# Layer 3's queries and keys: from one level of Strassen's method on two samples to two levels on four

## The chip, the cores and the metric

One core of a Trainium2 chip runs the whole kernel. Time is the device time of that core in microseconds (us). A profiled execution gives the trace behind every view; three plain executions give the times. TensorE is called PE in the views (PEld are its weight loads), VectorE DVE, ScalarE ACT, GpSimd POOL and the queue that issues the DMAs SP.

## The reference, cut to what matters

128 samples, each with x of 128 nodes by 512 features and an adjacency matrix of 128 by 128, pass four layers; each ends in `x = layernorm(x + layer(x, adj))`. All is fp32.

- Layer 0 mixes neighbours through a transition matrix in two steps, with three weight matrices.
- Layer 1 is a hypergraph convolution through 1024 hidden features.
- Layer 2 builds attention weights from one score per node, then multiplies by W.
- Layer 3, the one that is edited, is masked attention with 8 heads of 64:

```
q, k, v = x@Wq.T + bq, x@Wk.T + bk, x@Wv.T + bv      # per sample, 128 x 512 each
scores  = (q @ k.T) * 64**-0.5 * (adj + adj)         # per head, 128 x 128
ctx     = softmax(scores) @ v
x       = layernorm(x + ctx@Wo.T + bo)
```

## The kernel before, in words

The kernel works on pairs of samples (U = 2, 64 pairs). Three stages follow each other: `layer0` (four samples at a time), `layer1` and `layer23` (a pair at a time). A stage is a generator: each `yield` in it ends a step. `layer` (L1233) runs the steps of pair k with `plan.key = start + k + w`, w from the lists `WHEN0`, `WHEN1`, `WHEN2` (L35 to L38), so one unit of the key is one pair and several pairs are under way at once.

Nothing is issued while the steps run. `Plan.add` (L181) records each operation with its engine, an estimated duration and what it depends on. `Plan.order` (L227) then places all operations: PE takes the ready operation with the lowest key, the other engines the one that is due first (`deadlines`, L342). It also gives each tile its place: `slots` (L398) says how many places of a kind there are, and `later` which places are made out of others once those are done for good. `emit` writes the instructions out in that order, so all of them carry one line, L364. Each engine executes its list strictly in that order.

The kinds of tiles: "bank" is one of eight PSUM banks (two of them called t0 and t1), "four" holds 2 x 512 numbers per partition, "sq" 2 x 130, "row" 512, "col" 12, "out" layer 0's results. `first` is one large SBUF tensor that holds layer 0's weights and later w2 and the weights of q and k ("w28") and W ("w14").

`strassen` (L538) multiplies a 2 x 2 arrangement of blocks by another with 7 products in place of 8 (Winograd's form). `operands` (L523) makes four sums of the left blocks on POOL, `combine` (L469) the sums of the weights once. Three banks are used: al gathers four of the products one after the other, be two, ga one, and after each product an eviction adds the bank to a result in SBUF (`take`). With `flip` the weights stand still in PE and the left block moves, so that the result comes out transposed.

In `layer23`, a pair goes through these steps: x2 and adj are loaded; layer 2's weights F are made and go through DRAM to be transposed; GT = x2.T F; the product with W and the layer norm give x3, which stays in SBUF in the tile of x2 and also goes through DRAM, to come back as xT; POOL makes the sums for q, k and v, and adds the bias bo to x3; q and k come out of one `strassen` with `nk = 2, nh = 512, flip=True`: 7 products, each of 512 columns in 8 matmuls of 128 x 128 x 128; v, scores, softmax, ctx and the product with Wo follow, whose evictions start from x3.

`layer0` already multiplies four samples by two levels of the method: 49 products of 386 columns. Its sums of left blocks and its seven inner `strassen` calls are written out in that function.

Of the kernel before, what the change touches and what calls it, by code (L numbers as in the profile page):

```python
# [17 lines left out]
P = 128  # L18
D = 512
# [9 lines left out]
SQS = 13  # L29
COLS = 48  # L30
ROWS = 8
# [6 lines left out]
WHEN2 = (-2.4, -2.0, -1.45, -1.15, -.7, 0, .35, .7, 1.35, 1.7)  # L38
LAG1, LAG2 = 1, -.5
RAMP = 0, 0, .2, 6  # L40
# [19 lines left out]
SPARE, AHEAD = 3, 6  # L60
SIZE = {"four": U * D, "sq": U * (P + 2), "bank": D, "col": 12, "row": D, "w28": 7168, "w14": 3584,
        "w7": 7 * QW, "out": U * 4 * QW, "t0": D, "t1": D}
# [99 lines left out]
class Plan:  # L162
# [64 lines left out]
    def order(self, urgent=None):  # L227
# [40 lines left out]
        def look(e):  # L268
# [3 lines left out]
            for k, t in ready[e].items():  # L272
# [7 lines left out]
                for kind, tiles in new.items():  # L280
                    s, m = slots[kind], len(tiles)
                    spare = 0
                    if not all(tile in line[kind][-m:] for tile in tiles):
                        spare = SPARE if all(tile in line[kind][-m - AHEAD:] for tile in tiles) else math.inf
                    if len(s) < m + (min(spare, 3) if kind == "bank" else spare):
                        break
                    t = max(t, sorted(s)[m - 1][0])
                else:
                    can.append((rank[k], t, k))
                    if t < soonest:  # L290
                        soonest = t
# [81 lines left out]
def kernel(  # L373
# [16 lines left out]
    first = const.tile([P, 7 * SIZE["w7"]], FP, name="first")  # L390
    outs = [const.tile([P, SIZE["out"]], FP, name=f"out{k}") for k in range(OUTS)]
    places = {"w7": [first[:, k * SIZE["w7"]:(k + 1) * SIZE["w7"]] for k in range(7)], "out": outs}
    at = 3 * SIZE["w7"], 7 * SIZE["w7"] - SIZE["w14"]
    places["w28"] = [first[:, k:k + SIZE["w28"]] for k in (0, at[0])]
    places["w14"] = [first[:, at[1]:]]
    later = {("w28", 0): [("w7", k) for k in range(3)], ("w28", 1): [("w7", k) for k in range(3, 6)],
             ("w14", 0): [("w7", k) for k in range(5, 7)]}
    slots = {"w7": 7, "out": OUTS, "w28": 0, "w14": 0, "sq": SQS, "col": COLS, "row": ROWS, "bank": 6, "t0": 1, "t1": 1,  # L398
             "four": BUFS}
# [6 lines left out]
    for k, t in enumerate(outs):  # L406
        for c in range(SIZE["out"] // SIZE["four"]):
            later["four", len(places["four"])] = [("out", k)]
            places["four"].append(t[:, c * SIZE["four"]:(c + 1) * SIZE["four"]])
# [55 lines left out]
    def seven(nk, nh):  # L465

        return tile_of("w28" if nk * nh == 1024 else "w14", 7, nk, nh)
# [8 lines left out]
    def load_blocks(W, left, right, by_blocks=False, dma=sp.dma_start):  # L476


        for half, at in ((left, B11), (right, B12)):
            to = W[:, at:at + 2].rearrange("p g c f -> p (g c) f")  # L480
            if by_blocks:
                with plan.together():
                    for k in range(4):
                        dma(to[k * Q:(k + 1) * Q], half.rearrange("(k c a) f -> k a c f", k=4, a=Q)[k],
                            run=half.shape[1], parts=Q)
            else:
                dma(to, half.rearrange("(c p) f -> p c f", p=P))
        combine(W)

    def load_T(W, srcs, nk, nh, with_stage=None, by_blocks=False, scale=1.0):  # L490

        n = 0
        for src in srcs:
            for o in range(src.shape[0] // P):
# [11 lines left out]
                for g in range(src.shape[1] // D):  # L506
# [5 lines left out]
                    for c0 in range(0, C, nk):  # L512
# [4 lines left out]
                        ac.mul(W[:, blk, k0:k0 + m, at:at + P], pt[:, c0:c0 + m],  # L517
                               scale if src is srcs[0] else 1.0)
                n += P
                yield  # L520
        combine(W)
# [173 lines left out]

    def spread_pair(srcs):
# [34 lines left out]
    def prepare0():  # L731
# [56 lines left out]
        flat = [w.rearrange("p j o f -> p (j o f)") for w in W]  # L788
        for to, a, b in ((T1, B12, B11), (T2, B22, T1), (T3, T2, B11), (N4, B21, T2)):
            (po if to in (T3, N4) else ve).tensor_tensor(flat[to], flat[a], flat[b], OP.subtract)  # L790
# [23 lines left out]
    def layer0(i0):  # L814
# [10 lines left out]

        base = plan.key

        def sums(to, L):

            S1, S2, S3, S4 = (to[:, k] for k in range(4))  # L830
            po.tensor_tensor(S1, L[:, :, 1, 0], L[:, :, 1, 1], OP.add)
            po.tensor_tensor(S3, L[:, :, 0, 0], L[:, :, 1, 0], OP.subtract)
            po.tensor_tensor(S2, S1, L[:, :, 0, 0], OP.subtract)
            po.tensor_tensor(S4, L[:, :, 0, 1], S2, OP.subtract)

        halves_of = [t.rearrange("p u (j c) n -> p j u c n", j=2) for t in xT]
        (A11, A12), (A21, A22) = [[t[:, j] for j in range(2)] for t in halves_of]
        lefts = []

        def give(L, n):  # L840
            to = tile_of("four", 4, n, P)
            sums(to, L)
            lefts.extend((L[:, j], to[:, :, j]) for j in range(n))

        give(halves_of[0], 2)
        two = [tile_of("four", 2, U, 2, P) for _ in range(2)]
        (S2, S1), (S4, S3) = [[t[:, j] for j in range(2)] for t in two]
        po.tensor_tensor(S1, A21, A22, OP.add)
        po.tensor_tensor(S2, S1, A11, OP.subtract)
        plan.key = base + .5  # L850
        give(two[0], 2)
        plan.key = base + 1
        po.tensor_tensor(S4, A12, S2, OP.subtract)
        po.tensor_tensor(S3, A11, A21, OP.subtract)
        give(two[1], 2)
        plan.key = base + 1.5
        give(halves_of[1][:, 1:], 1)
# [5 lines left out]
        def quarters(r, half):  # L863

            return [R[r][:, b, 2 * half + n] for b in range(U) for n in range(2)]

        def fresh(d, bs):

            def put(d, b):
                def run(p):  # L870
                    ac.copy(d[:, P:], p[:, P:])
                    add(d[:, :P], p[:, :P], b, OP.add)
                return run
            d11, d12, d21, d22 = d
            return {"p1": put(d11, bs[:, 0]), "c11": lambda p: add(d11, p, d11, OP.add),
                    "v": put(d12, bs[:, 1]), "c12": lambda p: add(d12, p, d12, OP.add),
                    "p5": put(d22, bs[:, 1]), "c22": lambda p: add(d22, p, d22, OP.add),
                    "c21": put(d21, bs[:, 0])}

        C11, C12, X, Y = quarters(0, 0), quarters(0, 1), quarters(1, 0), quarters(1, 1)  # L880
        sides = [[R[r][:, b, 2 * h:2 * h + 2] for b in range(U)] for r, h in ((0, 1), (1, 0), (1, 1))]
        for k, (j, take) in enumerate((
                (B11, fresh(X, bias[:, 0])), (B21, biased_take(C11, X)), (T2, biased_take(X, X)),
                (T1, fresh(Y, bias[:, 1])), (B22, biased_take(C12, C12)), (T3, biased_take(X, X)),
                (N4, biased_take(X, X)))):
            plan.key = base + .28 * k
            L, S = lefts[k]
            strassen((L[:, 0, :1], L[:, 0, 1:], L[:, 1, 1:], [S[:, i:i + 1] for i in range(4)]), WT["0"][j], 1, QW,
                     take)
            if j in (T1, T3):  # L890
                for b in range(U):
                    po.tensor_tensor(sides[j == T3 and 2][b], sides[1][b], sides[2][b], OP.add)
# [41 lines left out]
    b1_b = [row() for _ in range(2)]  # L934
    b2h = row()
    bw2 = row()
# [25 lines left out]
    def layer1(i0):  # L962
# [23 lines left out]
        K = sq(M)  # L986
# [76 lines left out]
    def prepare2():  # L1063
# [15 lines left out]
        ve.tensor_copy(bkT, pt[:, C:2 * C])  # L1079
        yield  # L1080
        WT["w"] = seven(2, h)
        load_blocks(WT["w"], w[:, :h], w[:, h:])
        yield
        WT["qk"] = seven(2, D)
        yield from load_T(WT["qk"], [wq, wk], 2, D, None, True, 0.25)
# [17 lines left out]
    def layer23(i0):  # L1103
        x2 = load_rows(x2d[i0 // U])
        A = load_adj(i0)
        yield
        s2 = col(U)
        for b in range(U):
            dot(s2[:, b:b + 1], x2[:, b], wa_b)
        deg = col(U)  # L1110
        ve.tensor_reduce(deg, A, AX.X, OP.add)
        pt = spread_pair([s2[:, b:b + 1].to_broadcast([P, P]) for b in range(U)])
        F = sq()
        for b in range(U):
            ac.activation(F[:, b], pt[:, b * P:(b + 1) * P], AF.Tanh, bias=s2[:, b:b + 1])
        ac.activation(F, F, AF.Prelu, alpha=0.1)
        ac.activation(F, F, AF.Exp, scale=8.0)
        r = col(U)
        for b in range(U):
            ve.scalar_tensor_tensor(F[:, b], F[:, b], 1.0, A[:, b], op0=OP.mult, op1=OP.mult,  # L1120
                                           accum_out=r[:, b:b + 1])
        ve.reciprocal(r, r)
        for b in range(U):
            po.tensor_scalar(F[:, b], F[:, b], r[:, b:b + 1], deg[:, b:b + 1], op0=OP.mult, op1=OP.mult)
# [163 lines left out]
```

## Time and profile before

| what | value |
|---|---|
| median of 3 runs | 5561.65 us (5557.36 to 5562.09) |
| the profiled execution's own time | 5560.11 us |
| its span | 5558.2 us |
| PE busy | 5489.4 us, 28697 records |
| DVE, ACT, POOL busy | 3872.5, 2121.4, 3370.9 us |
| DMA | 650.24 MB, mean 117 GB/s |
| layers 2 and 3 | first store of the output at 3266 us, last at 5554 us |

The span is from the first instruction to the last in the profiled execution. A busy share is an average over three stages with different loads, so the shares are to be read stage by stage. Matmul ends are modelled, and an fp32 matmul leaves two records for itself and two for its weight loads. Idle time of an engine other than PE costs nothing unless PE waits for it.

### The profile page before, as it was taken

What the parts mean: (1) busy time and instruction counts of PE and PEld (TensorE: products, weight loads), DVE (VectorE), ACT (ScalarE), POOL (GpSimd) and SP (SyncE); (2) the same over time, 40 slices, a digit from 0 to 9 for tenths busy, and PEclk for the clock granted to TensorE, in tenths of its full rate; (3) what the DMA queues carried; (4) which work ended last, traced back from release to release, by engine and by line L of the source; (5) the groups of instructions that cost most, each with busy time, mean ns of one, the idle gap of its engine ahead of it and who ended that gap; (6) DMA issues with size and microseconds to landing.
All of it is one profiled execution on the core that took longest, in us unless ns stands there. A gap on an engine that the chain in (4) does not pass through costs nothing.

```text
span 5558.2 us, 87851 instructions
## 1 busy us (share of the span) xinstructions
PE 5489.4 (99%) x28697; PEld 4082.3 (73%) x28697; DVE 3872.5 (70%) x8130; ACT 2121.4 (38%) x5327; POOL 3370.9 (61%) x5080
## 2 busy tenths in 40 slices
PE   8999999999999999999999999999999999999999
PEld 4555555555666666666666798999999999999998
DVE  6888888878666666666665666767677777776766
ACT  2333333334333333333333333433333333333433
POOL 6767777766666666666666545555555555555554
PEclk9999999999999999999999999999999999999999
DMA  3333333334444443344444434434443344334442
GB/s 89 105 93 103 96 97 103 99 105 138 137 132 115 119 115 115 110 116 119 119 119 119 131 108 130 132 113 122 133 131 115 121 133 133 116 120 131 131 127 91
DMA packets 717680, 650.24 MB, mean 117 GB/s; under 512 B 259739, under 2 KB 571043, under 8 KB 717222
## 3 DMA queue, kind: packets, MB, share of 16 engines
q1 hardware_dynamic: 715718, 641.99, 39.0%
q8 instruction: 229, 3.75, 0.3%
q10 hardware_dynamic: 1504, 2.62, 0.2%
q14 instruction: 229, 1.88, 0.1%
HBM read 360.20 MB, written 284.16 MB: 116 GB/s over the span
## 4 chain that ended last, share of the span: by engine, by line
PE 85%; DMA 4%; DVE 4%; POOL 2%; issue 1%; SPq 1%; ACT 1%; DVEq 0%; ACTq 0%; POOLq 0%
PE bank L364 66%; PE t L364 19%; DVE out L364 2%; SPq L364 1%; DMA four<-x 1%; POOL four L364 1%; DMA four<-h 1%; DMA out<-h 1%; DVE col L364 1%; DVE four L364 1%; POOL out L364 1%; POOL col L364 1%; ACT out L364 1%; DVE sq L364 0%; DMA four<-in_x_dram 0%
## 5 line engine op out<-in xcount | busy, mean ns | idle before, releaser
L364 PE MATMUL bank<-first,four 128*128 128x386 f32 (+1 forms) x5372 | 1614.5, 447 | 21.7 <-DVE first L364 5.1
L364 PEld LDWEIGHTS bank<-first,four 128*128 128x128 f32 x5372 | 993.3, 190 | 583.3 <-DVE out L364 120.3
L364 DVE TENSOR_TENSOR out<-bank,out 128x386 f32<-128x386 f32 (+2 forms) x1785 | 913.6, 531 | 491.1 <-PE bank L364 423.5
L364 PE MATMUL bank<-four,four 128*64 128x128 f32 (+3 forms) x2508 | 598.1, 399 | 0.0
L364 POOL TENSOR_TENSOR four<-four 128x256 f32<-128x256 f32 (+2 forms) x502 | 360.4, 732 | 287.1 <-ACT four L364 187.0
L364 ACT COPY four<-bank 128x256 f32<-128x256 f32 (+1 forms) x494 | 233.3, 474 | 779.3 <-PE bank L364 775.8
L364 POOL TENSOR_TENSOR out<-out 128x772 f32<-128x772 f32 (+2 forms) x212 | 330.3, 1564 | 255.4 <-DVE out L364 214.7
L364 PEld LDWEIGHTS bank<-four,four 128*128 128x128 f32 (+2 forms) x2508 | 338.5, 172 | 188.2 <-issue 155.0
L364 DVE TENSOR_TENSOR four<-bank,four 128x256 f32<-128x256 f32 (+1 forms) x509 | 221.0, 437 | 346.0 <-PE bank L364 339.4
L364 POOL TENSOR_TENSOR four<-four,four 128x256 f32<-128x256 f32 (+2 forms) x566 | 447.1, 792 | 10.7
L364 POOL TENSOR_TENSOR out<-out,row 128x512 f32<-128x512 f32 x208 | 264.9, 1277 | 275.7 <-PE bank L364 116.0
L364 PE MATMUL bank<-four,first 128*128 128x128 f32 x3536 | 422.3, 275 | 0.7 <-DVE four L364 0.7
L364 PEld LDWEIGHTS bank<-four,first 128*128 128x128 f32 x3536 | 414.4, 192 | 7.1 <-DVE four L364 1.1
L364 ACT ACTIVATE out<-out,col,col 128x512 f32<-128x512 f32 (+1 forms) x290 | 280.1, 985 | 341.7 <-POOL col L364 331.4
L364 ACT COPY out<-bank 128x258 f32<-128x258 f32 (+2 forms) x484 | 194.4, 404 | 566.0 <-PE bank L364 451.2
L364 PE MATMUL bank<-first,out 128*128 128x256 f32 (+1 forms) x1748 | 407.5, 380 | 0.5 <-DVE out L364 0.3
L364 PE MATMUL bank<-four,out 128*128 128x512 f32 (+3 forms) x1500 | 402.8, 416 | 2.6 <-DVE four L364 2.6
L364 POOL TENSOR_SCALAR col<-col 128x1 f32<-128x1 f32 (+1 forms) x704 | 189.4, 273 | 351.9 <-DVE col L364 315.6
L364 ACT ACTIVATE four<-four,col,col 128x512 f32<-128x512 f32 (+1 forms) x350 | 285.4, 820 | 302.4 <-POOL col L364 267.1
L364 POOL TENSOR_TENSOR col<-col,neghalf 128x1 f32<-128x1 f32 x640 | 387.4, 609 | 17.0
L364 PE MATMUL bank<-out,four 128*128 128x256 f32 (+3 forms) x1768 | 363.0, 363 | 8.2 <-DVE out L364 6.2
L364 PEld LDWEIGHTS bank<-first,out 128*128 128x128 f32 x1748 | 330.5, 190 | 51.5 <-DVE out L364 2.9
(213 smaller groups left out, 10368.3 us busy)
## 6 DMA issues: line engine op xcount, KB each, us to landing
h<-out SPq DMA_DIRECT2D x472, 128.0 KB, 2.5
four<-S SPq DMA_DIRECT2D x76, 512.0 KB, 4.4
S<-four SPq DMA_DIRECT2D x75, 512.0 KB, 2.9
out<-h SPq DMA_DIRECT2D x69, 512.0 KB, 4.6
four<-in_x_dram SPq DMA_DIRECT2D x512, 64.0 KB, 2.1
four<-in_x_dram SPq DMA_DIRECT2D x62, 512.0 KB, 3.8
x1d<-four SPq DMA_DIRECT2D x62, 512.0 KB, 2.8
out<-x1d SPq DMA_DIRECT2D x59, 512.0 KB, 6.1
```

The costliest lines, as they stand in the source:

```text
L364: call(*map(real, args), **{n: real(a) for n, a in kw.items()})
```

## The change

The queries and keys of layer 3 are made for four samples (two pairs) at a time by two levels of the method: an outer level over the pair index and the two halves of q and k, an inner level in each of its seven products. That is 49 products with one contraction block of 128 and 256 columns, where two pairs had 14 products with two blocks and 512 columns.

- `lefts` and `twice` are layer 0's code, moved out into functions that layer 0 and `layer23` call. `lefts` makes the sums of both levels on POOL. `twice` runs the seven inner `strassen` calls; two POOL additions form the shared part of the results after the products T1 and T3.
- The weights of q and k lie in seven tiles "q7". `load_T(twice=True)` combines them at the inner level, `combine_once_more` at the outer.
- Evictions that carry a bias are two ACTIVATEs of 128 columns with the bias as a column, on ScalarE; the other 41 of 49 add the bank to the result on VectorE. The bias bk is stored as bk - bq.
- x3 is stored to DRAM (`x3d`) after layer 2 and reloaded for the product with Wo; bo is added after the reload. The results of that product are written over x3.
- `layer23` runs on two pairs, with a key per pair inside a step (`each`), and the attention is a function of its own, with times from `WHENV`, `WHENS`, `WHENP` and `WHENO`.
- Places: 8 in place of 13 sq, 32 of 48 col, 4 of 8 row and one "row1" for layer 1's rows; layer 1's K has a kind of its own with 4 places. After layer 1 the places of w2, row1 and K become fours. W is loaded into fours by `prepare_w`; Wv's and Wo's load (`prepare3`) has a later key.

```diff
-SQS = 13
-COLS = 48
-ROWS = 8
+SQS = 8
+COLS = 32
+ROWS = 4
+KS = 4
...
-WHEN2 = (-2.4, -2.0, -1.45, -1.15, -.7, 0, .35, .7, 1.35, 1.7)
-LAG1, LAG2 = 1, -.5
-RAMP = 0, 0, .2, 6
+WHEN2 = (-2.4, -2.0, -1.45, -1.15, -.7, .3, .5, 2)
+WHENV, WHENS, WHENP, WHENO = (.9, 1.9), (2.2, 3.2), (3, 4), (3.5, 4.5)
+LAG1, LAG2 = 1, -.25
+SOFT = .2
+RAMP = 0, 0, .05, 4
...
+    def lefts(xT, step=.5):
+        base = plan.key
+        def sums(to, L):
+            S1, S2, S3, S4 = (to[:, k] for k in range(4))
+            po.tensor_tensor(S1, L[:, :, 1, 0], L[:, :, 1, 1], OP.add)
+            po.tensor_tensor(S3, L[:, :, 0, 0], L[:, :, 1, 0], OP.subtract)
+            po.tensor_tensor(S2, S1, L[:, :, 0, 0], OP.subtract)
+            po.tensor_tensor(S4, L[:, :, 0, 1], S2, OP.subtract)
...
+        give(halves_of[0], 2)
+        two = [tile_of("four", 2, U, 2, P) for _ in range(2)]
+        (S2, S1), (S4, S3) = [[t[:, j] for j in range(2)] for t in two]
+        po.tensor_tensor(S1, A21, A22, OP.add)
+        po.tensor_tensor(S2, S1, A11, OP.subtract)
+        plan.key = base + step
+        give(two[0], 2)
+        plan.key = base + 2 * step
+        po.tensor_tensor(S4, A12, S2, OP.subtract)
+        po.tensor_tensor(S3, A11, A21, OP.subtract)
+        give(two[1], 2)
+        plan.key = base + 3 * step
+        give(halves_of[1][:, 1:], 1)
+        return found
+
+    def twice(left, W, width, quarters, sides, fresh, step, flip=False):
+        base = plan.key
+        C11, C12, X, Y = (quarters(r, half) for r in range(2) for half in range(2))
+        for k, (j, take) in enumerate((
+                (B11, fresh[0](X)), (B21, biased_take(C11, X)), (T2, biased_take(X, X)), (T1, fresh[1](Y)),
+                (B22, biased_take(C12, C12)), (T3, biased_take(X, X)), (N4, biased_take(X, X)))):
+            plan.key = base + step * k
+            L, S = left[k]
+            strassen((L[:, 0, :1], L[:, 0, 1:], L[:, 1, 1:], [S[:, i:i + 1] for i in range(4)]), W[j], 1, width,
+                     take, flip=flip)
+            if j in (T1, T3):
+                for d, v, y in zip(sides(*((0, 1), (1, 1))[j == T3]), sides(1, 0), sides(1, 1)):
+                    po.tensor_tensor(d, v, y, OP.add)
...
     def layer23(i0):
...
+            strassen(ops, WT["w"], 2, D // 2, normed(biased_take(halves(x2), halves(x2)), x2))
+
+            loads.append(through_dram(x2.rearrange("p b (k w) -> p b k w", k=4), f"x3{i}"))
+            x3ds.append(held(f"x3d{i}"))
+            sp.dma_start(x3ds[-1], x2)
...
-        strassen(ops, WT["qk"], 2, D, {
-            "p1": op(qT[:, 0], bqb), "c11": op(qT[:, 0], qT[:, 0]), "v": op(kT[:, 0], bkb),
-            "c12": op(kT[:, 0], kT[:, 0]), "p5": op(kT[:, 1], bkb), "c22": op(kT[:, 1], kT[:, 1]),
-            "c21": op(qT[:, 1], bqb)}, flip=True)
+        left = lefts(xT)
+        yield
+        qk = [[four().rearrange("p u (f n) -> p u f n", n=P) for _ in range(2)] for _ in range(2)]
...
+                    def run(p):
+                        for f in range(2):
+                            ac.activation(d[:, f * P:(f + 1) * P], p[:, f * P:(f + 1) * P], AF.Identity,
+                                          bias=bias[:, 2 * q + f:2 * q + f + 1])
...
+        twice(left, WT["qk"], 2 * P,
+              lambda r, half: [qk[r][half][:, b, 2 * m:2 * m + 2].rearrange("p f n -> p (f n)")
+                               for b in range(U) for m in range(2)],
+              lambda r, half: [qk[r][half][:, b].rearrange("p f n -> p (f n)") for b in range(U)],
+              [fresh(bqT), fresh(bkT)], .25, True)
+        for r in range(2):
+            plan.key = base + WHENV[r]
+            strassen(operands(*blocks(xT[r])), WT["v"], 2, D // 2, plain_take(*halves(vs[r])))
+        yield
+        for r, i in enumerate(both):
+            attention(i, As[r], *qk[r], vs[r], x3ds[r], base, r)
...
-        t = four()
-        yield
-        strassen(ops, WT["o"], 2, D // 2, normed(biased_take(halves(t), halves(x3)), t))
-        sp.dma_start(out[i0:i0 + U].rearrange("b p f -> p b f"), t)
+        plan.key = base + WHENO[r]
+        x3 = load_rows(x3d)
+        for b in range(U):
+            po.tensor_tensor(x3[:, b], x3[:, b], bo_b, OP.add)
+        strassen(ops, WT["o"], 2, D // 2, normed(biased_take(halves(x3), halves(x3)), x3))
+        sp.dma_start(out[i0:i0 + U].rearrange("b p f -> p b f"), x3)
```

## Prediction, before the result was known

> **What bounds the kernel now.** I read four views in this order: the page, the busy times of two stretches, the order of time inside one pair, and the groups by form. First the page (busy time, share of the span, instructions) and the chain that ended last:
>
> ```profile
> PE 5489.4 (99%) x28697; PEld 4082.3 (73%) x28697; DVE 3872.5 (70%) x8130; ACT 2121.4 (38%) x5327; POOL 3370.9 (61%) x5080
> PEclk9999999999999999999999999999999999999999
> PE 85%; DMA 4%; DVE 4%; POOL 2%; issue 1%; SPq 1%; ACT 1%; DVEq 0%; ACTq 0%; POOLq 0%
> ```
>
> TensorE is busy 99% of the span at full clock, and it is 85% of the chain. The average hides three stages, so next come the windows: one inside layer 0, which already uses 49 products per four samples, and one inside the stage that the change edits (layers 2 and 3, from about 3200 us to the end).
>
> ```profile
> core 0: us, PE busy (x) PEld busy (x) DVE busy (x) ACT busy (x) POOL busy (x), PEclk, DMA share, GB/s
> 500.00:1000.00 500.00, 497.20 (x1478) 267.15 (x1477) 399.30 (x936) 191.50 (x423) 358.22 (x499) 1.00 0.34 99
> 3300.00:5300.00 2000.00, 1990.30 (x15016) 1818.31 (x15015) 1422.42 (x2929) 777.90 (x2594) 1107.59 (x1623) 1.00 0.41 126
> ```
>
> In the edited stage TensorE idles 9.7 us of 2000 (0.49%), with DVE at 71% and POOL at 55%. Layer 0 idles 2.8 of 500 (0.56%) with DVE at 80% and POOL at 72%. So in both places matmul time is wall time. The stores of the output leave 36.77 us apart (mean over 48 pairs), 73.54 us per four samples. The timeline gives the price of one matmul:
>
> ```profile
> 4214.67 1.03 PE L364 MATMUL bank<-four,out 128*128 128x256 f32 x4
> 4215.54 1.03 PE L364 MATMUL t<-out,out 128*128 128x256 f32 x4
> 4226.90 1.95 PE L364 MATMUL bank<-out,first 128*128 128x128 f32 x16
> 4228.69 3.74 PE L364 MATMUL bank<-four,first 128*128 128x128 f32 x32
> 4232.26 1.95 PE L364 MATMUL bank<-out,first 128*128 128x128 f32 x16
> ```
>
> Each fp32 matmul leaves two records. From start to start, 16 records of 128 columns take 1.79 us (4226.90 to 4228.69) and 32 take 3.57, so one 128-column matmul costs 0.223 us. A 256-column one costs 0.87/2 = 0.433 us.
>
> **The change part by part.**
>
> *TensorE.* Before, a pair of samples has 7 products, each of 4 (f) x 2 (c) = 8 matmuls of 128 columns: 56, or 112 per four samples. After, four samples have 49 products of 2 matmuls of 128 columns: 98. The kind is the same (a 128x128 weight load, 128 moving columns). So 14 x 32 groups = 448 matmuls go (the two programs hold 14565 and 14117): 448 x 0.2234 = 100.1 us, on the path. No other matmul is added or removed.
>
> *VectorE and ScalarE.* Rows for the evictions and sums (mean ns is the figure behind the busy time):
>
> ```profile
> L364 DVE TENSOR_TENSOR four<-bank,four 128x256 f32<-128x256 f32 x475 | 197.6, 419 | 320.8 <-PE bank L364 314.2 <-POOL sq L364 2.0 <-POOL out L364 0.8
> L364 DVE TENSOR_TENSOR out<-bank,bqT 128x512 f32<-128x512 f32 x64 | 44.2, 690 | 69.7 <-PE bank L364 69.6
> L364 ACT ACTIVATE sq<-bank,col 128x128 f32<-128x128 f32 x210 | 66.2, 363 | 115.8 <-PE bank L364 114.0 <-ACT four L364 1.7
> L364 POOL TENSOR_TENSOR four<-four,four x566: 452/730/1287, 15.1 to 5532.5; 128x256 f32<-128x256 f32 x136, 128x512 f32<-128x512 f32 x31, 128x128 f32<-128x128 f32 x22
> L364 POOL TENSOR_TENSOR out<-out 128x512 f32<-128x512 f32 x60 | 76.4, 1275 | 26.0 <-DVE out L364 18.2 <-DMA out<-x1d 6.4 <-DMA sq<-in_adj_dram 0.8
> ```
>
> Removed per four samples: 14 evictions of 512 (0.690). Added: 41 of 256 on DVE (0.419) and, for the eight evictions that carry a bias, 16 ACTIVATEs of 128 (0.363). DVE: 17.2 - 9.7 = +7.5 us. It has 52.3 now (1422.4/2000 x 73.54), so it comes to 59.8 of a period of 73.54 - 3.13 = 70.4 us, 85%. ACT: 28.6 + 5.8 = 34.4 us, 49%.
>
> *POOL.* Added per four samples: 12 sums of 256 (0.73), 4 of 128 (0.459, mean of that shape in the trace), 4 of 512 (1.275) for the left operands, and 4 of 512 for the shared halves of q and k: 8.8 + 1.8 + 5.1 + 5.1 = +20.8 us. POOL has 40.7 now, so it comes to 61.5 of 70.4 us, 87%. No stage of the trace runs POOL or DVE this full; layer 0 is nearest. These loads are shadowed by TensorE as long as they arrive in time. The bounds on added TensorE idle: below, 0 (or the 11 us idle now, if mixing helps); above, the second rival. I take layer 0's rate as a floor and 1% as a ceiling of the likely case, 12.6 to 22 us of 2250 against 11.5 now: +1 to +11, middle +6. A hint for the low end: after, the qk matmuls stand in TensorE's order in runs of mostly 2 to 16 between products of w, v and o and the scores, where before they stood in runs of 40 and more. An eviction of 0.42 us thus has 256-column products (0.87 us each) beside it.
>
> *DMA and SP.* Two DMAs of 512 KB per pair are new: the store of x3 and its reload, 128 in all, 67 MB. The DMA share of this stage goes from 0.41 to about 0.50, worked out by bytes. The store stands on SP's queue behind the eight pieces of x3, which wait for the same layer norm; the S and F transfers are behind it. The reload is issued right before or inside the next x3 pieces, one group after its store. If that cover were gone, the o evictions would wait for 6.6 us (median landing of the like load of x2d) plus 2 x 1.28 us of POOL for bo, which moves with it at no change in count. Cost taken: 0; bounds -1 and +1.6 us per pair, where +1.6 x 64 would eat the gain.
>
> *The other edits.* Fewer sq, col and row tiles and the K tiles of their own change the order in layers 0 and 1 little: TensorE's order in layer 1 is the same run by run (2, 16, 8, 28 matmuls per pair). The weights of qk now take 16 combines of 256 and 4 of 1792 on DVE in place of 4 of 1024, some 10 us more, once, in layer 1, where DVE is at 61%. W's load moves later, beside layer 1's last pairs. Together 0, bounds -3 and +5 us. The tail: from the last qk matmul (5513.2 us) to the end is 45.0 us now with some 30 us of matmuls. After, 27 us of matmuls follow the last qk (S, C, S, 14 of v or o, 16 transposes, C, 28 of o), and two pairs' softmaxes queue on DVE and ACT. By the rows this chain is about 40 us, so idle stays near 13: 0, bounds -5 and +8.
>
> *Sum.* The profiled execution took 5560.1 us (span 5558.2), 1.5 below the median of 5561.65. 5560.1 - 100.1 + 6 = 5466.0; against the median 5467.
>
> **A rule that speaks against it.** The trace shows POOL stretched while VectorE runs an operation with two SBUF inputs (here the dot product into junk):
>
> ```profile
> 4227.71 0.93 DVE L364 SCALAR_TENSOR_TENSOR junk<-out,row 128x512 f32<-128x512 f32 x1
> 4228.06 0.66 POOL L364 TENSOR_SCALAR col<-col 128x1 f32<-128x1 f32 x1
> 4228.82 0.68 POOL L364 TENSOR_SCALAR col<-col,col 128x1 f32<-128x1 f32 x1
> ```
>
> 0.66 against a typical 0.25. The Trainium skill, "GPSIMD Engine Reference", section Specifications, says that POOL shares its SBUF interfaces with VectorE and contends with two-SBUF-input instructions. Over all records, POOL operations that meet such an instruction take 850 instead of 729 ns (256 elements), 541 instead of 248 (column scalar) and 1002 instead of 563 (column power). If the rule bit everywhere, POOL's 61.5 us per group would gain 36 x 0.12 + 8 x (2 x 0.29 + 0.44) and some 2 us on the other forms, less 1.6 already in the means: some 74.2 us, more than the 73.5 of today. But the new evictions read PSUM and one SBUF tensor, and only 44 of the 1408 sums of 256 met a two-input instruction. I use the rows.
>
> **The rivals.**
>
> 1. *Likeliest (0.74): the matmuls go, little comes in their place.* 5455 to 5485.
>
> 2. *Evictions starve TensorE (0.17).* A qk product is now 0.447 us, not 1.79, and four of the seven in each inner scheme add up in one bank, so each waits for the eviction before it: 0.42 us plus two handovers of about 0.2. For: DVE at 85%, eight banks. Against: layer 0 does the same at 0.56% idle, with products of 0.65 us. If in three of the seven inner schemes one step finds only one product to cover those 0.82 us, 3 x 0.4 x 32 = 38 us: 5505; range 5485 to 5530.
>
> 3. *POOL becomes the bound (0.06), the slower side.* Place: the left sums in front of each group's qk products, queued with the layer norms' column operations and the softmax scaling. Price: 32 x (POOL's time per group - 70.4). It decides from 73.5 us, 12 us above my sum. At the rule's 74.2 the time is 5560 + 22 = 5582. For: 87% load. Against: the overlap counts above.
>
> 4. *It gains a little more (0.03):* waits fall, 5443 to 5455. That the count does not fall is excluded by the two programs.
>
> **How the numbers follow.** The time is the first case's, 5467. Leaving out 5450 and below (0.03) and the top of cases 2 and 3 (0.12) gives 5450 to 5515. A measurement of this kernel can tell about 0.2% (11 us) from no change: faster needs less than 5550. Cases 1, 2 and 4 lie there nearly whole (0.92); same 0.03; slower 0.05.
>
> **What would show it.** Right: 448 fewer matmuls, 128-column qk matmuls still at 0.223 us, output stores about 70.4 us apart per four samples, TensorE idle below 1% in the stage, POOL near 87%, DVE near 85%. Wrong: TensorE waits for VectorE of over 60 us in the stage (case 2), or waits for POOL on tiles of the left sums with POOL above 95% (case 3), or for the reload of x3 on SP.

## The result, and the profile after

| | before | changed |
|---|---|---|
| median of 4 runs each | 5560.94 us (5557.36 to 5562.09) | 5500.13 us (5494.10 to 5502.76) |
| the profiled execution | 5560.11 us, span 5558.2 | 5494.10 us, span 5492.0 |

The ratio is 0.989 (95% interval 0.9873 to 0.9907). The change gains 60.8 us, where 94 were forecast. The 100 us of matmuls went, but 39 us came back by the medians (35 by the profiles below), 33 more than the 6 of the forecast; these 33 are what the expectations speak of. A second set of runs, the base of the experiments, gave 5495.08 us against 5558.93 (0.9886, 0.9871 to 0.9901), a gain of 63.9 us, so some 3 us between sets mean nothing.

The page of the changed kernel, its busy row, clock row and chain:

```profile
PE 5408.3 (98%) x27801; PEld 4003.2 (73%) x27801; DVE 4015.5 (73%) x9010; ACT 2255.4 (41%) x5839; POOL 3993.5 (73%) x5848
PEclk9999999999999999999999999999999999999999
PE 87%; DVE 4%; DMA 3%; POOL 2%; issue 2%; ACT 1%; SPq 1%; DVEq 0%; POOLq 0%; ACTq 0%
```

Records fell from 28697 to 27801, which is 896, two for each of 448 matmuls. The clock is unchanged. The busy times of the same two stretches:

```profile
core 0: us, PE busy (x) PEld busy (x) DVE busy (x) ACT busy (x) POOL busy (x), PEclk, DMA share, GB/s
500.00:1000.00 500.00, 497.39 (x1475) 266.53 (x1474) 398.76 (x930) 190.23 (x419) 356.56 (x491) 1.00 0.35 100
3300.00:5300.00 2000.00, 1994.32 (x14776) 1813.34 (x14775) 1576.89 (x3779) 923.86 (x3137) 1684.19 (x2353) 1.00 0.52 160
```

In the edited stage TensorE idles 5.7 us of 2000, less than the 9.7 before, and yet it does less per microsecond than it could. The longest waits that the steady part shows from 3500 to 5200 us (what waited, for what; us in total, times, longest) are next to nothing, first the longest of before, then the three longest of the changed kernel:

```profile
engine line waited for: us in total, times, longest us
PE bank L364 <- POOL out L364: 3.7, 6, 0.8
PE bank L367 <- DVE out L367: 0.9, 3, 0.4
PE bank L367 <- DVE four L367: 0.6, 2, 0.4
PE bank L367 <- ACT four L367: 0.4, 1, 0.4
```

So most of the lost time of the steady part lies inside instructions that count as busy. To see it, I priced every matmul record by its undisturbed distance to the next, from the trace of before (0.112 us for 128 columns, 0.216 for 256, 0.324 for 386, 0.429 for 512, 0.0575 and 0.0549 for the scores' and context's half tiles). All records together cost 5400.7 us before and 5300.3 after. What the real distances have above that is "lost" time, whether the views call it idle or busy. It includes the changes of tile shape, which before has too. The table splits it at three events that every kernel has: the last matmul of layer 0, the scores of the 9th pair and the scores of the 57th.

| us lost | to layer 0's end | to pair 9 | 48 pairs | the rest | sum |
|---|---|---|---|---|---|
| before | 72.1 | 29.4 | 33.0 | 18.1 | 152.6 |
| changed | 75.9 | 33.6 | 46.4 | 32.0 | 187.9 |
| difference | +3.8 | +4.2 | +13.4 | +13.9 | +35.3 |

The changed row is that of the second set's profile; the first profile gives 75.0, 35.0, 45.4 and 31.2, so about 1.5 us in a cell means nothing. Between sets the second column can differ more: two runs below lose 4 to 5 us more than the base by 3100 us, where every engine still has the base's order of instructions.

### The profile page after: what moved, and what is told of

Read it like the earlier page. It is cut to its first block, busy times and chain, and to the rows that moved or that the text cites. A ratio compares the mean times of both kernels' runs of the same rounds, so it can differ in the third digit from the quotient of the medians.

```text
span 5492.0 us, 88697 instructions
## 1 busy us (share of the span) xinstructions
PE 5408.3 (98%) x27801; PEld 4003.2 (73%) x27801; DVE 4015.5 (73%) x9010; ACT 2255.4 (41%) x5839; POOL 3993.5 (73%) x5848
## 4 chain that ended last, share of the span: by engine, by line
PE 87%; DVE 4%; DMA 3%; POOL 2%; issue 2%; ACT 1%; SPq 1%; DVEq 0%; POOLq 0%; ACTq 0%
PE bank L367 66%; PE t L367 20%; DVE out L367 2%; SPq L367 1%; DVE col L367 1%; DMA out<-h 1%; DVE four L367 1%; ACT out L367 1%; POOL col L367 0%; POOL out L367 0%; POOL four L367 0%; DVE first L367 0%; DVE sq L367 0%; DMA four<-in_x_dram 0%; POOL first L367 0%
## 5 line engine op out<-in xcount | busy, mean ns | idle before, releaser
L367 DVE TENSOR_TENSOR out<-bank,out 128x386 f32<-128x386 f32 (+1 forms) x1949 | 951.1, 506 | 524.8 <-PE bank L367 444.0
L367 PE MATMUL bank<-first,four 128*128 128x386 f32 (+3 forms) x4416 | 1292.8, 446 | 25.4 <-DVE out L367 10.1
L367 PEld LDWEIGHTS bank<-first,four 128*128 128x128 f32 (+2 forms) x4416 | 744.5, 189 | 550.8 <-DVE out L367 129.2
L367 PE MATMUL bank<-four,out 128*128 128x256 f32 (+2 forms) x2100 | 707.7, 474 | 0.3 <-DVE four L367 0.2
L367 POOL TENSOR_TENSOR out<-out 128x256 f32<-128x256 f32 (+3 forms) x424 | 492.8, 1173 | 253.3 <-DVE out L367 202.7
L367 PEld LDWEIGHTS bank<-four,out 128*128 128x128 f32 (+1 forms) x2100 | 375.9, 190 | 253.4 <-issue 208.3
L367 PE MATMUL bank<-first,out 128*128 128x256 f32 (+3 forms) x2168 | 469.2, 372 | 1.6 <-DVE out L367 1.1
L367 PEld LDWEIGHTS bank<-first,out 128*128 128x128 f32 (+2 forms) x2168 | 387.1, 188 | 56.2 <-DVE out L367 3.0
L367 PE MATMUL bank<-out,first 128*128 128x128 f32 (+3 forms) x2192 | 344.9, 298 | 1.8 <-DVE out L367 0.7
L367 PE MATMUL bank<-four,first 128*128 128x128 f32 (+3 forms) x1612 | 317.3, 331 | 1.8 <-DVE out L367 1.5
```

The source lines that it names most:

```text
L367: call(*map(real, args), **{n: real(a) for n, a in kw.items()})
```

## The experiments

All runs are of the changed kernel with the edit that is shown. They fall into three sets, each on another chip and with its own runs of the kernel before. The base, the two runs with one kind of work made thin and the second level taken back have 5558.93 us for before. The tile shape, the start, the end's keys and all three edits have 5562.78. Both at once, the new keys alone, the thin end and the better version have 5559.52. A comparison across sets is therefore given as the gain over the set's own before, where the base has 63.9 us.

**The base.**

> The changed kernel once more, as the base for the runs beside it: 5495 to 5503 us by every theory.

Measured: 5495.08 us (5493.99 to 5498.75).

**Less work in the same order.** The planner works with full durations and so gives the same order; only at the end, when the instructions are written, are the marked ones made narrower. What changes is the load of the marked engines.

```diff
+THIN = (POOL,)
...
+                if k in self.thinned:
+                    args = [narrow(a) for a in args]
...
+    return v[(slice(None),) * v.idx.ndim + (slice(0, v.shape[-1] // 8),)]
...
+        plan.thin = True
         left = lefts(xT)
+        plan.thin = False
...
+        plan.thin = True
         twice(left, WT["qk"], 2 * P,
```

> The changed kernel, with the instructions in the same order on every engine, but the POOL additions for q and k (the sums of the left blocks and the shared halves after T1 and T3) are done on one eighth of their columns, so that part of the computation is left out. Theory 'POOL's load': if some of the 33 us of TensorE time that came back are waits for POOL's 20.8 us per four samples, they go: 5480 to 5490 us. Theory 'turnaround of the banks' (short products, each waiting for the eviction before it) and theory 'order of the instructions' (start, tail, switches of the tile shape): POOL is not on the path in the steady part, 5495 to 5503 us.

Measured: 5481.07 us (5479.98 to 5484.83), 14.0 less than the base. POOL's load does hold TensorE up.

For the evictions the mark stands around `twice` alone and `THIN = DVE, ACT`.

> The changed kernel, with the instructions in the same order on every engine, but the 49 evictions per four samples of the products of q and k (VectorE's additions and ScalarE's with a bias) are done on one eighth of their columns, so that part of the computation is left out. Theory 'turnaround of the banks': the short stalls inside the q and k products in the steady part (149 of about 87 ns in 1700 us, against 46 before) go, 9 to 14 us in all: 5484 to 5492 us. Theory 'POOL's load' and theory 'order of the instructions': less than 4 us, 5493 to 5503 us.

Measured: 5482.07 us (5478.34 to 5488.97), 13.0 less: this theory holds too. The place shows in the timelines (start, us busy, instruction group, records). First the changed kernel, from the last record of a pair's scores on:

```profile
start us, us, engine line op out<-in xcount [idle before <-releaser]
4205.68 0.27 PE L367 MATMUL t<-first,four 64*128 64x128 f32 x1
4205.88 0.71 PE L367 MATMUL t<-first 128*128 128x128 f32 x4
4206.43 0.61 PE L367 MATMUL bank<-first 128*128 128x128 f32 x4
4206.88 0.61 PE L367 MATMUL bank<-rows,first 128*128 128x128 f32 x4
4207.32 0.61 PE L367 MATMUL bank<-first 128*128 128x128 f32 x4
4207.77 1.21 PE L367 MATMUL bank<-rows,first 128*128 128x128 f32 x8
4208.82 1.03 PE L367 MATMUL bank<-four,first 128*128 128x256 f32 x4
```

Then the same place with thin evictions, from the first record behind the scores on:

```profile
4195.85 0.71 PE L373 MATMUL t<-first 128*128 128x128 f32 x4
4196.40 0.61 PE L373 MATMUL bank<-first 128*128 128x128 f32 x4
4196.84 0.61 PE L373 MATMUL bank<-rows,first 128*128 128x128 f32 x4
4197.29 0.61 PE L373 MATMUL bank<-first 128*128 128x128 f32 x4
4197.74 1.06 PE L373 MATMUL bank<-rows,first 128*128 128x128 f32 x8
4198.63 1.03 PE L373 MATMUL bank<-four,first 128*128 128x256 f32 x4
```

A product of q and k is four records, 0.45 us from start to start. Where eight come together, the next group starts after 1.05 us in the changed kernel and after 0.89 with thin evictions. The view calls neither an idle gap; the stall only makes the group's busy time longer (1.21 for 1.06). Over the 48 pairs such stalls of more than 40 ns inside products of 128-column matmuls number 0 before, 86 (6.8 us) in the changed kernel and 3 (0.6 us) with thin evictions; with POOL thin they stay at 86. Products of 256 columns have 34 such stalls (9.6 us) before, 43 (6.4 us) in the changed kernel, 37 with thin evictions and 26 (3.8 us) with POOL thin. So the short products of q and k wait for their evictions, and POOL's load shows elsewhere. The first record behind a pair's scores or context products is left out of these counts. It is late in every run alike, thin or not (0.55 us to the next group from 4205.88 and from 4195.85), and belongs to the change of tile shape below.

**Both at once**, `THIN = DVE, ACT, POOL`.

> The changed kernel in its own order, with both the POOL additions for q and k and the 49 evictions of their products per four samples done on one eighth of their columns (that part of the computation is left out). Theory 'two terms': POOL's load (14.0 us when it alone was thinned) and the turnaround of the banks (13.0 us) add: 5466 to 5471 us. Rival 'one shared term' (either shortens the same chain from the left sums to the evictions, or relieves the same engine): about as with one of them, 5477 to 5483 us. What stays in both cases is the order: one more change of the tile shape per pair (0.09 us x 64 = 6 us) and the end.

Measured: 5471.21 us (5468.06 to 5473.11), 23.9 less than the base, of 27.0 if they added fully (24.5, by the gains over before). They are mostly two terms. The table shows where the three runs lose less than the base, by their profiles:

| us less lost | to layer 0's end | to pair 9 | 48 pairs | the rest |
|---|---|---|---|---|
| POOL thin | 1.8 | 4.3 | 3.5 | 3.4 |
| evictions thin | 1.2 | 8.2 | 6.0 | 1.6 |
| both thin | 0.2 | 14.6 | 7.5 | 4.8 |

The largest part lies ahead of the 9th pair, where both thin lose only 19.0 us and before itself lost 29.4. So the 24 us are not a share of the 35 that the change brought: thin work also takes away waits that the kernel before has. In the 48 pairs the two loads are worth 7.5 us.

**The second level taken back.** q and k by the old `strassen` in each pair, all else as in the changed kernel:

```diff
-        twice(left, WT["qk"], 2 * P,
...
+            plan.key = base + WHEN2[6] + r
+            qT, kT = qk[r]
+            strassen(ops, WT["qk"], 2, D, {
```

> The changed kernel's steps, keys and places (groups of four samples, x3 stored and reloaded, W in fours, the late load of Wv and Wo), but q and k by one level as before: 7 products of 512 columns per pair, in place of the 49 of 256 per four. TensorE has the 100.1 us of matmuls again. Theory 'order of the instructions': the regrouping alone costs most of what came back, at the start of the last stage, at its end and at the tile switches: about 5561 + 20 to 33 = 5581 to 5594 us. Theory 'turnaround of the banks' or 'POOL's load': the regrouping is free and the second level's short products cost it: 5557 to 5568 us.

Measured: 5596.70 us (5595.27 to 5603.58), 37.8 above before and 101.6 above the base, just over the interval that 'order' gave. But not by its reasons: to pair 9 the loss is 26.5 us, less than before, and in the rest it is 23.8, between before and the changed kernel. The 48 pairs lose 62.6 us, mostly inside and between products of 256 columns. The waits on top from 3500 to 5200 us did not stand there before:

```profile
PE bank L367 <- DVE col L367: 11.1, 18, 0.6
PE t L367 <- DVE col L367: 3.2, 5, 0.7
```

That keys which suit short products don't suit long ones is a reading, not shown. The run doesn't isolate the regrouping, and I draw nothing from its total.

**The tile shape.** Before, the scores (64-row tiles) stood directly ahead of the context products (64-column tiles), three changes of shape in a pair. In the changed kernel other products stand between them, four changes. The edit moves the context products' keys and then closes the gap in the finished order where nothing depends on it:

```diff
-WHENV, WHENS, WHENP, WHENO = (.9, 1.9), (2.2, 3.2), (3, 4), (3.5, 4.5)
+WHENV, WHENS, WHENP, WHENO = (.9, 1.9), (2.2, 3.2), (3.19, 4.19), (3.5, 4.5)
...
-        for k in sorted(range(len(start)), key=lambda k: (start[k], k)):
+        for k in self.beside(sorted(range(len(start)), key=lambda k: (start[k], k)), place):
...
+            line[p:q] = [k for k in line[p:q] if k not in late] + late
```

> The changed kernel with the scores (S, 16 matmuls on 64-row tiles) of one pair put directly behind the context products (C, 16 matmuls on 64-column tiles) of the pair before it, in 56 of 64 pairs; in the changed kernel one to six other products of 128x128 tiles stand between them, so that TensorE changes the tile shape four times per pair in place of three. Theory 'a change of the tile shape costs about 90 ns of exposed weight load': 56 x 0.09 = 5 us less, 5488 to 5492 us, and about 0.1 us less lost per pair in the trace. Rival 'the switches cost nothing of their own': 5493 to 5499 us.

Measured: 5559.34 us (5553.91 to 5563.40), 64 slower than the base (a gain over before of 3.4 in place of 63.9), a miss by every theory. A second run has the new keys alone, without the move.

> The keys of the run with the scores directly behind the context products (WHENP at 3.19 and 4.19 in place of 3 and 4), but in the order that the planner gives them, one to four other products left between the two. That run took 5559 us, 64 us more than the changed kernel. Theory 'the move did it' (C and its evictions are late, and VectorE, which executes strictly in order, holds up the evictions behind them): 5498 to 5510 us. Rival 'the key did it' (the planner's whole order is worse): 5545 to 5562 us.

Measured: 5526.81 us (5522.43 to 5530.66), between the two. By the gains over before, the keys cost 31 us and the move 29 more. The price of a change of shape itself can be read in the traces, and it has two halves. The last record ahead of a change starts 90 to 100 ns further from the next than it would inside its group, and the first record behind it (into half tiles, the first two together) takes another 50 to 104 ns more. In the changed kernel's lines above, records of the scores start in twos every 0.11 us, the last is 0.20 ahead of the next product, and that product takes 0.55 us where its neighbours take 0.45. The weight loads go with this: inside a product of 128 columns a load starts about 109 ns ahead of its matmul, and at each change of the 48 pairs it starts only 1 to 2 ns ahead, so that no matmul hides it. Before, the same place reads:

```profile
4205.45 0.27 PE L364 MATMUL t<-out,out 64*128 64x128 f32 x1
4205.65 1.09 PE L364 MATMUL bank<-out,four 128*64 128x128 f32 x16
4206.57 1.04 PE L364 MATMUL bank<-four,four 128*64 128x128 f32 x16
4207.55 2.05 PE L364 MATMUL bank<-out,first 128*128 128x128 f32 x16
4209.43 1.03 PE L364 MATMUL bank<-four,four 128*128 128x256 f32 x4
```

The 16 records behind the context products take 1.88 us there, and 1.79 in the prediction's lines. Apart from four places before that also wait, these additions vary by a few ns over the 48 pairs, and they are the same in the thinned runs. Per pair the changes cost 0.54 us before, 0.74 in the changed kernel and again 0.54 with the move, twice what was expected for the fourth change (0.19 in place of 0.09). So the fourth change is 9.3 us of the 13.4 that the 48 pairs lose more; the stalls in 128-column products are 6.8, and everything else together fell by 2.7. The move does win back the 9.3 us, but with new keys and move together the 48 pairs lose 96.2 us in place of 46.4. Its waits in the steady part:

```profile
PE bank L390 <- DVE out L390: 11.2, 22, 1.1
PE bank L390 <- DVE four L390: 4.8, 11, 0.9
PE bank L390 <- DVE first L390: 4.0, 11, 0.6
```

TensorE waits for evictions on VectorE. That the delayed context products hold these up is a reading, not shown.

**The start of the stage.** In the changed kernel TensorE waits there for VectorE's dot product into junk, which belongs to the load of Wv and Wo:

```profile
PE bank L367 <- DVE junk L367: 2.9, 2, 2.5
```

```diff
-                             (prepare3, 2 * n + LAG1 - .1, .1)):
+                             (prepare3, 2 * n + LAG1 - .95, .05)):
```

> The changed kernel with the load and combination of Wv and Wo at its old key (2n + LAG1 - .95 in steps of .05, in place of - .1 in steps of .1). Theory 'start': most of the 16 us that TensorE loses more than before between 3000 and 3500 us are waits for this VectorE and POOL work (TensorE waits for the dot product into junk 3 times, 7 us), which then lies under layer 1: 5483 to 5489 us. Rival 'the first group of four starts late whatever the load does': 5493 to 5499 us.

Measured: 5506.48 us (5504.78 to 5511.98), 11 slower (7.6, by the gains over before). The wait for junk is gone, and a longer one stands in its place:

```profile
PE bank L367 <- ACT four L367: 6.4, 1, 6.4
```

To pair 9 it loses 41.1 us in place of 33.6, but 5.0 of these 7.5 are there by 3100 us, ahead of the first instruction that stands elsewhere than in the base. The theory 'start' is not borne out: an earlier load doesn't make the start faster.

**The end.** The last qk product completes q and k of two pairs at once, so two softmaxes follow it, with little for TensorE beside them. The changed kernel's timeline:

```profile
5453.07 1.03 PE L367 MATMUL t<-out,first 128*128 128x256 f32 x4
5454.89 1.10 PE L367 MATMUL t<-four,out 128*128 128x256 f32 x4 [0.80 <-DVE col L367]
5462.05 1.11 PE L367 MATMUL t<-ident,four 128*128 128x128 f32 x4 [6.06 <-POOL four L367]
5462.96 1.06 PE L367 MATMUL bank<-ident,four 128*128 128x128 f32 x4
5465.45 1.97 PE L367 MATMUL bank<-ident,out 128*128 128x128 f32 x8 [1.44 <-POOL out L367]
```

Other keys for the last group:

```diff
-            plan.key = base + WHENV[r]
+            plan.key = base + (WHENV, (2.1, 2.2))[i0 + 2 * U == B][r]
...
-        plan.key = base + WHENS[r]
+        plan.key = base + (WHENS, (1.7, 2.05))[i0 + (2 - r) * U == B][r]
```

> The changed kernel with other keys in the last group of four alone: the scores of its first pair at 1.7 (in place of 2.2), ahead of the last products of q and k, those of its second pair at 2.05 (of 3.2), and v at 2.1 and 2.2 (of .9 and 1.9), so that v's and o's products lie beside the two softmaxes. Theory 'tail': the 14 us that TensorE loses more than before behind the 56th pair are two softmaxes that queue one behind the other with nothing beside them, 6 to 10 us of which go: 5485 to 5489 us. Rival 'the end is a chain of softmax, context and o anyway': 5493 to 5499 us.

Measured: 5493.97 us (5492.57 to 5495.33), 1.1 less than the base; by the gains over before (68.8 and 63.9) it is 5 less, within the intervals of the two ratios. The trace agrees with the 5: the 6.06 us wait is gone, and the rest loses 26.9 us in place of 32.0. The stretch up to pair 9 loses 39.3 in place of 33.6, but the order of every engine is the base's up to 5389 us, so this difference is not the edit's.

The softmaxes of the last two pairs were also thinned in the unchanged order (`plan.thin = i0 + 2 * U >= B` behind the scores).

> The changed kernel in its own order, with the softmax of the last two pairs (VectorE, ScalarE and POOL between the scores and the turned weights) on one eighth of its columns, so that part of the last four samples' result is left out. Theory 'two softmaxes at the end': of the 32 us that TensorE loses behind the 56th pair 8 to 12 go: 5483 to 5488 us. Rival 'the end waits for something else' (evictions, transposes, layer norm): 5491 to 5498 us.

Measured: 5492.88 us (5488.69 to 5494.53), 2.2 less, no gain that can be told. The two waits shrink to 3.39 and 0.77 us, and no more:

```profile
5461.80 1.12 PE L373 MATMUL t<-ident,four 128*128 128x128 f32 x4 [3.39 <-POOL four L373]
5464.53 1.97 PE L373 MATMUL bank<-ident,out 128*128 128x128 f32 x8 [0.77 <-POOL out L373]
```

Seven eighths of the columns are under half of these two waits. What makes up the rest was not separated; the number of instructions and their handovers stay the same in this run.

**All three edits of order.**

> The three edits of the neighbouring runs together (scores directly behind context products, the early load of Wv and Wo, the keys of the last group). If the three terms add: 5468 to 5478 us; if they are the same waits seen from different places: 5482 to 5490 us.

Measured: 5539.32 us (5537.80 to 5543.12), worse than either expectation. The tile-shape edit alone costs more than the three together.

**A better version.** The keys of the end, and a planner that may give out places further ahead:

```diff
-SPARE, AHEAD = 4, 6
+SPARE, AHEAD = 4, 8
```

> An attempt at a better version: the changed kernel with the last group's keys of the run on the end, and with the planner allowed to give out places eight tiles ahead of the line in place of six (AHEAD). If an earlier start of work frees VectorE and POOL near the start of the stage: 5483 to 5490 us; if every such redrawing moves the waits only: 5492 to 5503 us.

Measured: 5474.27 us (5471.66 to 5476.92), ratio to before 0.9848 (0.9834 to 0.9861), better than both kernels. Its own loss table is 80.6, 21.1, 43.0 and 19.6, in sum 164.3. Against the run with the keys of the end alone (5493.97), AHEAD brings 19.7 us (16.4 by the gains over before, 23 by the two profiles). By the profiles most of it lies up to pair 9 (39.3 to 21.1, of which some 5 are the other run's, see above) and at the end (26.9 to 19.6), 3.8 in the 48 pairs, while layer 0 loses 6.0 more. The kernel before was not run with AHEAD at 8, so nothing shows that this gain belongs to the change. Its window:

```profile
3300.00:5300.00 2000.00, 1998.12 (x14822) 1818.36 (x14819) 1570.43 (x3786) 935.96 (x3143) 1673.36 (x2353) 1.00 0.52 159
```

Its loads on VectorE (1570 us) and POOL (1673) are those of the changed kernel; the order differs from 63 us on.

## Why the prediction was right and where it was off

The direction and the range were right, and so was the first rival's main step: the matmuls went, and their time with them. The point was 33 us too low. The time lies outside the first rival's own range (5455 to 5485) and inside the second's (5485 to 5530), so that the wide range held was in part luck: most of what came back has other causes than the second rival names.

- *TensorE, -100.1 us: right.* 448 matmuls went, and a 128-column one still takes 0.223 us (0.45 us per product of two). The stores leave 71.33 us apart per four samples, where 70.4 were forecast.
- *VectorE and ScalarE: right in count, a little high in sum.* 41 evictions of 256 came and 14 of 512 went. VectorE is at 79% (85% forecast), ScalarE at 46% (49%). VectorE gained back time that I hadn't looked for, see the last section.
- *POOL: right.* 84% against 87%, and one sum of 256 takes 737 ns in the 48 pairs, 729 before. The third rival's 73.5 us per group are far (60.1 by the window). The stretch to 74.2 us, the case of the rule that speaks against the forecast, did not come.
- *The added idle, +6 with bounds +1 to +11: the step that failed.* From the end of layer 0 to the last qk matmul 23.6 us more are lost: 4.2 up to pair 9, 13.4 in the 48 pairs and 6.0 behind them. I took layer 0's idle share as the floor and "idle" as the measure, and visible idle time indeed fell. The loss of the 48 pairs sits in busy time. 9.3 us of it are the fourth change of tile shape in a pair, which the prediction doesn't have at all. The stalls of short products are 6.8, and everything else together fell by 2.7. The cause of the 4.2 and the 6.0 stays open, apart from seven more changes of shape in the 4.2, some 1.3 us.
- *The second rival was partly true.* Evictions and handovers do hold up short products that share a bank: 86 stalls came, and all but 3 go when the evictions are thin. But they are 6.8 us in the 48 pairs, not the 38 of its estimate for the stage. Thin evictions give 13.0 us in all and less load on POOL gives 14.0, though at 84% it is not the bound; these gains count waits that before has too. The "hint for the low end" (256-column products stand between) was true of most products, not of all.
- *The tail, 0 with bounds -5 to +8: too low, at the upper bound.* From the last qk matmul to the end are 49.7 us, where I forecast about 40. TensorE loses 20.6 us there (21.5 in the base), 13.6 before, so 7 to 8 more. That two softmaxes queue was in the text; that 8.3 us of TensorE waits (0.80, 6.06, 1.44) follow was not in the sum. With keys of its own for the last group 13.5 us are lost from there on, but 13.4 ahead of it in place of 10.5, so 5 us less in all.
- *The other edits, 0: low.* Up to the end of layer 0 3.8 us more are lost; this was not tested. The planner's SPARE also went from 3 to 4, and no run isolates that.
- *The reload of x3, 0: right as far as seen.* No wait of TensorE for a DMA stands in the steady part. A version that keeps x3 in SBUF was not tried, as the kernel has no places left for it.

Open: why AHEAD helps just there, and whether it would help the kernel before as well. That it lets work for the first groups begin earlier is my reading of the table, not shown.

## What to carry to other kernels

When matmuls are removed from a kernel that TensorE bounds, price every remaining record by its undisturbed distance and sum what is above it: a share of busy time near 100% hides stalls. Count the changes of tile shape before and after: one more per pair cost more here than the stalls of the short products. An engine's load is priced by making its instructions narrower in an unchanged order, but the gain then includes waits that were there before the change. After a change of instruction sizes a planner's own constants are worth a try (here 16 to 23 us), and the kernel before should be given the same try, which was not done here. When runs come from several sets, compare each with its own set's before.

## What the runs showed of the hardware that was not expected

**Stalls in busy time.** The busy time of a group of eight records holds its stall (1.21 us for 1.06). The Trainium skill, "Perfetto Trace Analysis", section Identifying the Most-Contended Engine, says that matmul busy time is no good measure of how near TensorE is to its limit. The traces agree: in the window from 3300 to 5300 us visible idle time fell from 9.7 to 5.7 us, while the loss per pair rose from 0.69 to 0.97 us.

**A change of tile shape** costs 0.14 to 0.20 us in these traces: 90 to 100 ns ahead of it and 50 to 104 ns in the first record or two behind. The skill's "TensorEngine Tiling (Array Packing)", section Key Properties, says that a change of mode drains TensorE, without a figure. The group at 4205.88, just behind scores, takes 0.55 us to the next where its neighbours take 0.45, and it starts 0.20 us behind the last scores, which start in twos every 0.11.

**VectorE is stretched by POOL, not only POOL by VectorE.** VectorE's product of two SBUF tensors in layer 2, by form, before and after (3500 to 5200 us):

```profile
L364 DVE SCALAR_TENSOR_TENSOR sq<-sq,sq 128x128 f32<-128x128 f32 x92 | 65.9, 751 | 2.7
L367 DVE SCALAR_TENSOR_TENSOR sq<-sq,sq 128x128 f32<-128x128 f32 x94 | 25.0, 303 | 62.2 <-ACT sq L367 62.2
```

The mean fell from 751 to 303 ns with POOL busier. Of the 92 before, 58 overlapped a POOL instruction and took 1026 ns, the other 34 took 282. The POOL instruction was in every case an addition of 512 columns with a row. After, 18 of 94 overlap, only with sums of 256 columns, and take 362; the other 76 take 289. The new order keeps them apart from the long additions. This is 1.8 us per four samples of VectorE time, and a part of why VectorE stands at 79% and not at 85%.
